# An expert block as one object around the last attention: one batch element's routing computed before the attention's second half, its outputs computed beside the other batch element's norms

## The chip, the core and the metric

The kernel runs on one core of a Trainium2 chip. The metric is the device time in microseconds (us) of one execution. The core has five engines that matter here, each with its own instruction queue that is worked off in order: PE (TensorE: matrix products, weight loads and transposes), DVE (VectorE), ACT (ScalarE), POOL (GpSimd) and SP (which issues most transfers). Engines wait for each other on semaphores.

## What is computed

Eight residual steps over `x` of shape 2 x 512 x 512 (two batch elements of 512 rows). Each step adds a block's output, computed from the layer norm of `x`:

```python
x = x + L0_attn_a(layernorm(x)); x = x + L0_ffn(layernorm(x))
x = x + L0_attn_b(layernorm(x)); x = x + L0_ffn(layernorm(x))
x = x + L1_attn_a(layernorm(x)); x = x + L1_ffn(layernorm(x))
x = x + L1_attn_b(layernorm(x)); x = x + L1_ffn(layernorm(x))
```

The change touches the last three lines' `L1_ffn` (called twice, with the same weights) and the place where `L1_attn_b` is called between the two. `L1_ffn` is a base product plus a mixture of eight experts of rank 16, of which each row takes the best two:

```python
probs = softmax(x_flat @ W_router.T)                  # 8 experts
topk_probs, topk_idx = top_k(probs, 2)
topk_probs = topk_probs / sum(topk_probs)
combine = einsum('nk,nke->ne', topk_probs, one_hot(topk_idx, 8))
h = einsum('nd,erd->ner', x_flat, A)
expert_out = einsum('ner,eor->no', h * combine[:, :, None], B) * 2
out = x_flat @ W_base.T + b_base + expert_out
```

`L1_attn_b` is a causal multi-head attention with 32 heads of 16, with rotary positions, biases and an output product.

## The kernel before

**Tiles.** `x` lies in SBUF as eight tiles `x[0..7]` of 128 rows x 512 (four of batch element 0, four of batch element 1; `NT` is 4, `NTILES` 8). `k.xT[b]` holds the normalised, transposed rows of batch element `b`, from which all products read; it is a part of a tile named `room`. All data are float32, and a float32 matmul stands as two records in the trace.

**Layer norm of one tile** (`layernorm`, lines 171 to 204): DVE takes statistics (L172, L174, L208), POOL makes the inverse square root (L210), DVE writes `xn` (L182), POOL adds the next block's output bias to `x` (L215, where a bias is given), PE makes four transposes into a PSUM bank (L195), and ACT copies the bank into `xT` (L200).

**`ffn_moe`** (line 1310) is called twice, once before the last attention and once after it. It loads its weights (`w` the base weights, 1 MB; `war` the experts' first factors with the router beside them; `wb` the second factors), a bias row and a row `c_order`. For each tile there is a `front` and a `back`:

- `front(t)` (L1339 to L1369): four matmuls of 128 x 136 into a bank of the tag `pj` (there are two such banks), then on DVE the routing: the maximum of the 8 logits (L1345), on ACT the exponential (L1347), and again on DVE two rounds of maximum, comparison, first hit and mask (L1330 to L1336), the renormalisation (L1353 to L1361) and last the product of the 128 expert columns with their weights, `hw` (L1363). That is 16 DVE instructions, nearly all on 8 elements or one per partition, each waiting for the one before. The `pj` bank is read by L1363 and is free only after it.
- `back(t)` (L1371 to L1381): one transpose of `hw` (L1374), an ACT copy `hT` (L1376), four matmuls of 128 x 512 with `w` and one with `wb` into a bank of the tag `sc`, the add to `x[t]` on DVE (L218), and in the last call the transfer of `x[t]` to the output (L1381).

In both calls the loop of lines 1384 to 1393 goes front 0; norm 4; front 1; norm 5, back 0; and so on, so that norms of batch element 1 lie among the fronts of element 0. The norms of element 0 were made before the call.

**`attn_mha`** (line 1479) runs `prepare(b)` and `core(b)` for b = 0, 1. `prepare` makes queries and keys with their rotation (PE, ACT, DVE, POOL, then transfers from `room` into the padded head tiles `qs` and `ks`, L1528) and the values (`values`, L1543, with the DVE add L1547). `core(b)` stands inside a `tc.If` on a register; only its causal branch runs with these inputs. It scores (L1575 on PE, with a maximum on DVE at L1585), transposes the maxima (L1599), scores again transposed (L1611), takes exponentials on ACT (L1621), multiplies by the values (L1636), and ends with the output product (L162) and four adds to `x` (L218). Between `prepare(1)` and `core(1)` the four norms of batch element 0 for the following block are called (lines 1680 to 1683). A `tc.If` is a border for the scheduler: what is called before it stands before it in every engine's queue.

**Order.** A scheduler places the instructions of straight-line parts; within `core` the order on PE is written out by hand. The pools of SBUF: `w8` has five 1 MB buffers, `w3` six smaller ones, `bias` one; the small tiles of `ffn_moe` come from a pool `f1` with three buffers each, opened at each call.

Of the kernel before, what the change touches and what calls it, by code (L numbers as in the profile page):

```python
# [31 lines left out]
F32 = mybir.dt.float32  # L32
# [5 lines left out]
B, S, D = 2, 512, 512  # L38
P = 128
NT = S // P  # L40
# [5 lines left out]
class Block:  # L46


    def __init__(self, ctx, tc, x, out):
        nc = self.nc = tc.nc  # L50
        self.tc = tc
        self.out = out
        pool = lambda name, bufs, **kw: ctx.enter_context(tc.tile_pool(name=name, bufs=bufs, **kw))
        self.const = pool("const", 1)
        self.w = pool("w", 2)
        self.work = pool("work", 2)
        self.small = pool("small", 6)
        self.psum = pool("psum", 2, space=bass.MemoryType.PSUM)
        self.turns = 0
        self.held = None  # L60
        self.coef = None

        self.x = [
            self.const.tile([P, D], F32, tag=f"x{t}", name=f"x{t}") for t in range(NTILES)
        ]
        self.source = x
        self.load_x(0)


        self.room = self.const.tile([P, 4 * KC * S], F32, tag="room", name="room")  # L70
        parts = self.room.rearrange("p (n c s) -> p n c s", n=4, c=KC)
        self.xT = [parts[:, b] for b in range(B)]
        self.spare = [parts[:, 2 + i] for i in range(2)]
        self.spare_turn = 0
        self.ident = self.const.tile([P, P], F32, tag="ident", name="ident")
        make_identity(nc, self.ident)
        self.mhalf = self.const.tile([P, 1], F32, tag="mhalf", name="mhalf")
        nc.gpsimd.memset(self.mhalf, -0.5)
        self.ones = self.const.tile([P, 1], F32, tag="ones", name="ones")
        nc.gpsimd.memset(self.ones, 1.0)  # L80
# [642 lines left out]
class AdaptedBlock:  # L723
# [3 lines left out]
    R = 48  # L727
# [579 lines left out]
        k.release()  # L1307


def ffn_moe(k, a, last=False, beside=lambda t: None):  # L1310

    nc, tc = k.nc, k.tc
    E, R = 8, 16
    with ExitStack() as ctx:
        lp = ctx.enter_context(tc.tile_pool(name="f1", bufs=3))
        w = k.load(a["f1_w"], [P, KC, D], "w8", 5)
        war = k.load(a["f1_ar"], [P, KC, E * R + E], "w3", 6)
        wb = k.load(a["f1_b"], [P, D], "w3", 6)  # L1320
        bias = k.load_row(a["f1_bias"], D, "bias")
        order = k.load_row(a["c_order"], E, "c_order")

        for t in range(NT):
            k.add_bias(t, bias)

        def best(p, name):

            top = k.sm(1, name)
            nc.vector.tensor_reduce(top, p, AX.X, ALU.max)  # L1330
            cand = lp.tile([P, E], F32, tag="cand", name="cand")
            nc.vector.scalar_tensor_tensor(cand, p, top, order, ALU.is_equal, ALU.mult)
            first = k.sm(1, "first")
            nc.vector.tensor_reduce(first, cand, AX.X, ALU.max)
            hot = lp.tile([P, E], F32, tag="hot" + name, name="hot" + name)
            nc.vector.tensor_scalar(hot, cand, first, None, ALU.is_equal)  # L1336
            return top, hot

        def front(t):  # L1339
            b, cols = t // NT, bass.ts(t % NT, P)  # L1340
            ps = k.proj()
            k.chain(ps[:, : E * R + E], [(k.xT[b][:, c, cols], war[:, c]) for c in range(KC)])
            logits = ps[:, E * R : E * R + E]
            nmax = k.sm(1, "nmax")
            nc.vector.tensor_reduce(nmax, logits, AX.X, ALU.max, negate=True)  # L1345
            p = lp.tile([P, E], F32, tag="p", name="p")
            nc.scalar.activation(p, logits, AF.Exp, bias=nmax, scale=1.0)  # L1347
            p1, hot1 = best(p, "p1")
            rest = lp.tile([P, E], F32, tag="rest", name="rest")
            nc.vector.scalar_tensor_tensor(rest, hot1, -2.0, p, ALU.mult, ALU.add)  # L1350
            p2, hot2 = best(rest, "p2")
            both = k.sm(1, "both")
            nc.vector.tensor_tensor(both, p1, p2, ALU.add)  # L1353
            inv = k.sm(1, "inv")
            nc.vector.reciprocal(inv, both)
            c1 = lp.tile([P, E], F32, tag="c1", name="c1")
            nc.vector.tensor_scalar(c1, hot1, p1, None, ALU.mult)
            c2 = lp.tile([P, E], F32, tag="c2", name="c2")
            nc.vector.scalar_tensor_tensor(c2, hot2, p2, c1, ALU.mult, ALU.add)
            comb = lp.tile([P, E], F32, tag="comb", name="comb")  # L1360
            nc.vector.tensor_scalar(comb, c2, inv, 2.0, ALU.mult, ALU.mult)  # L1361
            hw = lp.tile([P, E, R], F32, tag="hw", name="hw")
            nc.vector.tensor_tensor(  # L1363
                hw,
                ps[:, : E * R].rearrange("p (e r) -> p e r", e=E),
                comb.unsqueeze(2).broadcast_to([P, E, R]),
                ALU.mult,
            )
            return hw  # L1369

        def back(t, hw):  # L1371
            b, cols = t // NT, bass.ts(t % NT, P)
            tp = k.tr()
            nc.tensor.transpose(tp[:, :P], hw.rearrange("p e r -> p (e r)"), k.ident)  # L1374
            hT = lp.tile([P, P], F32, tag="hT", name="hT")
            nc.scalar.copy(hT, tp[:, :P])  # L1376
            ps = k.sc()
            k.chain(ps, [(k.xT[b][:, c, cols], w[:, c]) for c in range(KC)] + [(hT, wb)])
            k.add_to_x(t, ps)
            if last:  # L1380
                nc.sync.dma_start(out=k.out[t], in_=k.x[t])  # L1381

        rows = {}
        for t in range(NTILES + 1):
            if t < NTILES:
                rows[t] = front(t)
                beside(t)
            if t < NT:
                k.layernorm(NT + t, bias=bias)
            if t > 0:  # L1390
                back(t - 1, rows.pop(t - 1))
            if t > NT and not last:
                k.layernorm(t - 1 - NT)


class CausalBound:
# [12 lines left out]
    def begin(self, n):  # L1409
        k = self.k  # L1410
        self.w = k.load(self.a["h_w" + n], [P, KC, D], "w8", 5)
        self.row = k.w.tile([P, D], F32, tag="bias", name="bound", bufs=1)
        k.nc.sync.dma_start(out=self.row[:1], in_=self.a["h_r" + n])
# [23 lines left out]
    def end(self):  # L1437
        k, nc = self.k, self.k.nc
        norm = self.norms[0]
        nc.vector.tensor_tensor(norm, norm, self.norms[1], ALU.mult)  # L1440

        nc.vector.tensor_scalar(norm, norm, self.LIMIT, None, ALU.is_lt)
        every = k.sm(1, "ve")[:1]
        nc.vector.tensor_reduce(every, norm, AX.X, ALU.min)
        self.flag = k.const.tile([1, 1], I32, tag="bound_flag", name="bound_flag")
        nc.vector.tensor_copy(self.flag, every)
# [29 lines left out]
        pool.memset(self.nm[i // 4][:, i % 4], 0.0)  # L1476


def attn_mha(k, a, exact, rooms):

# [1 line left out]
    nc, tc = k.nc, k.tc  # L1484
# [4 lines left out]
    with ExitStack() as ctx:  # L1489
        lp = ctx.enter_context(tc.tile_pool(name="h", bufs=2))  # L1490
# [12 lines left out]
        rows = [slice(32 * g, 32 * g + 32) for g in range(4)]  # L1503
# [29 lines left out]
        def prepare(b):  # L1533
            rotated(b, wq, bq, q, (nc.sync, nc.sync))
            if b == 0:
                for t in range(NT, NTILES):
                    k.layernorm(t, bias=bo)
            last = rotated(b, wk, bk, kk, (nc.sync, nc.scalar))

            with tc.issue_after(last):  # L1540
                values(b)
# [136 lines left out]
        for b in range(B):  # L1678
            prepare(b)
            if b:  # L1680

                for t in range(NT):
                    k.layernorm(t)
            with tc.If(exact != 0) as branch:
                core(b, True)
            with branch.Else():
                core(b, False)


@with_exitstack  # L1690
def kernel(ctx: ExitStack, tc: tile.TileContext, a: dict, out: bass.AP):
    k = Block(ctx, tc, a["x"], out)
    k.hold()
    block = attn_latent_small(k, a)
    bound = CausalBound(k, a)
    attn_gqa(k, a, bound, block)
    ffn_lora(k, a)
    attn_mla(k, a)
    with k.tc.tile_pool(name="heads", bufs=1) as pool:
        rooms = HeadRooms(k, a, pool)  # L1700
        ffn_moe(k, a, beside=rooms.fill)
        attn_mha(k, a, bound.register(), rooms)
    ffn_moe(k, a, last=True)

# [154 lines left out]
```

## Time and profile before

| what | value |
|---|---|
| time, three runs | 2104.93, 2110.02, 2113.53 us (median 2110.02) |
| the profiled execution: its own time | 2103.46 us |
| its span, first to last instruction | 2101.4 us |
| mean granted clock of PE | 0.992 |
| PE busy | 2031.9 us (97%) |
| DVE busy | 1351.0 us (64%) |
| ACT, POOL busy | 745.4 us (35%), 970.4 us (46%) |

Busy shares are means over stages that differ; a PE that is busy by its records is not always at its peak. In the views, "idle before <- X" is what ended an engine's wait, the chain of waits is the work that ended last followed back from the last instruction, and the granted clock says which share of full speed PE was given in a stretch. The stages around the change lie as follows in the trace: first expert block 1689 to 1742 us, attention of batch element 0 from 1742 to 1891, `prepare(1)` from 1891 to 1932, `core(1)` from 1935 to 2040, second expert block from 2043 to the end.

### The profile page before, as it was taken

How to read it: one execution, taken by the hardware profiler on the slowest of the kernel's cores; microseconds unless marked ns; L12 is line 12 of the kernel's file. 1: busy time of each engine (PE TensorE's matmuls, PEld its weight loads, DVE VectorE, ACT ScalarE, POOL GpSimd, SP SyncE). 2: the span in 40 equal slices, each digit the busy share in tenths (PEclk: the TensorE clock that was granted, in tenths of full speed). 3: DMA queues.
4: the chain of work that ended last, by engine and by line, in shares of the span. 5: the costliest groups of instructions: out<-in, count | busy, mean ns of one | idle time of the engine just before them, and what ended most of it. 6: DMA issues, size and time to landing. Idle time of an engine off the chain costs nothing. (4 is left out here: it accounts for less than half of the span.)

```text
span 2101.4 us, 40138 instructions
## 1 busy us (share of the span) xinstructions
PE 2031.9 (97%) x15560; PEld 1147.1 (55%) x15560; DVE 1351.0 (64%) x3575; ACT 745.4 (35%) x2072; POOL 970.4 (46%) x1239
## 2 busy tenths in 40 slices
PE   9999999999999999999999989999999999999998
PEld 5444435666666566666665544545454454654654
DVE  7678766756566566666664557666666784855845
ACT  3555632222222222222222145444544411441531
POOL 1101016776555557566653246555555555115220
PEclk9999999999999999999999999999999999999999
DMA  3001012222222222222220321010101003002001
GB/s 100 16 21 41 1 66 76 72 76 71 91 71 71 91 71 76 71 91 76 73 77 26 117 61 54 22 51 25 50 22 52 2 6 70 2 2 41 2 2 40
DMA packets 70221, 107.43 MB, mean 51 GB/s; under 512 B 13699, under 2 KB 50691, under 8 KB 63237
## 3 DMA queue, kind: packets, MB, share of 16 engines
q1 hardware_dynamic: 69380, 103.71, 15.6%
q8 instruction: 126, 2.06, 0.4%
q10 hardware_dynamic: 640, 1.05, 0.3%
q14 instruction: 75, 0.61, 0.1%
HBM read 80.61 MB, written 2.10 MB: 39 GB/s over the span
## 5 line engine op out<-in xcount | busy, mean ns | idle before, releaser
L263 ACT ACTIVATE room<-room,nmax 128x128 f32<-128x128 f32 (+3 forms) x384 | 212.3, 555 | 484.2 <-DVE nmax L253 482.7
L274 POOL TENSOR_SCALAR room<-room,invs 128x128 f32<-128x128 f32 (+3 forms) x384 | 198.0, 537 | 142.1 <-DVE invs L271 142.1
L314 PE MATMUL sc<-turned,vals 32*128 32x128 f32 (+7 forms) x1034 | 186.2, 411 | 1.3 <-DVE turned L287 1.3
L314 PE MATMUL pj<-turned,vals 32*128 32x384 f32 (+7 forms) x708 | 184.9, 422 | 0.0
L210 POOL TENSOR_TENSOR rstd<-ve,mhalf 128x1 f32<-128x1 f32 x80 | 45.9, 577 | 246.0 <-DVE ve L208 240.2
L314 PE MATMUL tp<-turned,vals 32*128 32x256 f32 (+7 forms) x770 | 147.1, 420 | 2.5 <-DMA vals<-v 2.1
L242 PE MATMUL sc<-kT,q 128*32 128x256 f32 (+4 forms) x1528 | 134.0, 384 | 6.8 <-DVE invs L271 4.1
L287 DVE STREAM_TRANSPOSE turned<-room 128x1152 f32<-128x1152 f32 x80 | 109.1, 1363 | 42.4 <-POOL room L274 39.9
L314 PEld LDWEIGHTS sc<-turned,vals 32*128 32x128 f32 (+1 forms) x1034 | 119.3, 166 | 14.3 <-issue 4.2
L943 POOL TENSOR_TENSOR q<-q,cosq 128x512 f32<-128x512 f32 x60 | 89.5, 1491 | 59.9 <-DVE t L940 59.9
L162 PE MATMUL sc<-w,room 128*128 128x512 f32 (+1 forms) x256 | 112.1, 582 | 0.0
L314 PEld LDWEIGHTS pj<-turned,vals 32*128 32x128 f32 (+1 forms) x708 | 104.0, 169 | 4.0 <-issue 1.6
L314 PEld LDWEIGHTS tp<-turned,vals 32*128 32x128 f32 (+1 forms) x770 | 97.6, 169 | 10.8 <-issue 4.9
L162 PE MATMUL sc<-w,ctxT 128*128 128x512 f32 x224 | 101.5, 596 | 0.0
L218 DVE TENSOR_TENSOR x<-sc,x 128x512 f32<-128x512 f32 x79 | 54.2, 686 | 73.0 <-PE sc L162 70.3
L242 PE MATMUL tp<-kT,q 128*32 128x512 f32 (+4 forms) x984 | 91.7, 407 | 4.5 <-DVE invs L271 3.8
L274 POOL TENSOR_SCALAR probs<-probs,invs 128x128 f32<-128x128 f32 (+3 forms) x128 | 65.8, 535 | 65.0 <-DVE invs L271 61.2
L263 ACT ACTIVATE probs<-probs,nmax 128x128 f32<-128x128 f32 (+3 forms) x128 | 71.1, 556 | 65.5 <-DVE nmax L253 64.3
L253 DVE CUSTOM_DVE_ANT_0 room<-sc,mask 128x256 f32<-128x256 f32 (+3 forms) x149 | 70.7, 474 | 35.6 <-PE sc L242 34.1
L242 PE MATMUL pj<-kT,q 128*32 128x288 f32 (+3 forms) x968 | 89.6, 404 | 2.9 <-POOL q L1211 1.9
L944 POOL TENSOR_TENSOR q<-q,t 128x512 f32<-128x512 f32 x64 | 88.0, 1374 | 6.5 <-DVE q L943 2.5
L1208 POOL TENSOR_TENSOR t<-t,sinq 128x512 f32<-128x512 f32 x32 | 40.8, 1276 | 106.4 <-DVE invs L271 100.6
(621 smaller groups left out, 6232.9 us busy)
## 6 DMA issues: line engine op xcount, KB each, us to landing
w<-in_b_wq SPq DMA_DIRECT2D x16, 1024.0 KB, 4.9
w<-in_b_wo SPq DMA_DIRECT2D x16, 1024.0 KB, 5.2
vals<-v SPq DMA_DIRECT2D x256, 64.0 KB, 2.0
w<-in_m_wo SPq DMA_DIRECT2D x8, 1024.0 KB, 7.2
w<-in_b_wk SPq DMA_DIRECT2D x16, 256.0 KB, 2.5
w<-in_b_wupv SPq DMA_DIRECT2D x16, 256.0 KB, 2.5
w<-in_f_w SPq DMA_DIRECT2D x4, 1024.0 KB, 6.0
w<-in_m_wqn SPq DMA_DIRECT2D x8, 384.0 KB, 3.1
```

The source lines that it names most:

```text
L162: last = self.nc.tensor.matmul(out, lhsT, rhs, start=(i == 0), stop=(i == len(pairs) - 1))
L210: self.nc.gpsimd.tensor_tensor(r, ve, self.mhalf, ALU.pow)
L218: self.latest = self.nc.vector.tensor_tensor(self.x[t], ps, self.x[t], ALU.add).ins
L242: nc.tensor.matmul(ps[32 * i : 32 * i + 32, a - lo : b - lo], q[:, at : at + 32], keys[:, a:b], start=True, stop=True,)
L253: nc.vector.tensor_tensor_reduce(out=row, in0=ps[:, :kv], in1=self.mask_back[:, :kv] if qt % 2 else self.mask[:, S - kv :], op0=ALU.add, o ...
L263: nc.scalar.activation(row, row, AF.Exp, bias=nmax, scale=-1.0, accum_out=total[:, qt : qt + 1])
L274: self.nc.gpsimd.tensor_scalar(row, row, inv[:, qt : qt + 1], 1.0, ALU.mult, ALU.mult)
L287: self.nc.vector.transpose(out[:, :last], probs[:, :last])
L314: self.nc.tensor.matmul(out[:, :, :n], values(i, j), rhs, start=(j == blocks[0]), stop=(j == stop[i]),)
L943: mul.tensor_tensor(q, q, tables["cosq"], ALU.mult)
L944: nc.gpsimd.tensor_tensor(q, q, t2, ALU.add)
L1208: nc.gpsimd.tensor_tensor(t2, t2, sinq, ALU.mult)
```

## The change

`ffn_moe` becomes a class `Experts`, built once ahead of both uses, so that the weights, `c_order` and the small tiles live through the attention (pool `f1` now with two buffers each, `hw` with four). Its `front` and `back` are the same instructions as before. `first` is the old first call. The old second call is split: `begin`, called between `prepare(1)` and `core(1)`, makes the norms of batch element 0 as before and directly after each norm its front; `end`, after the attention, makes for each t a norm of element 1, the back of element 0 and the front of element 1, and then the four backs of element 1.

```diff
-def ffn_moe(k, a, last=False, beside=lambda t: None):
...
-        lp = ctx.enter_context(tc.tile_pool(name="f1", bufs=3))
+class Experts:
...
+    def __init__(self, k, a, lp):
...
         w = k.load(a["f1_w"], [P, KC, D], "w8", 5)
         war = k.load(a["f1_ar"], [P, KC, E * R + E], "w3", 6)
         wb = k.load(a["f1_b"], [P, D], "w3", 6)
-        bias = k.load_row(a["f1_bias"], D, "bias")
         order = k.load_row(a["c_order"], E, "c_order")
...
-            hw = lp.tile([P, E, R], F32, tag="hw", name="hw")
+            hw = lp.tile([P, E, R], F32, tag="hw", name="hw", bufs=4)
...
+    def begin(self):
+        self.added = self.bias()
+        for t in range(NT):
+            self.k.layernorm(t, bias=self.added)
+            self.front(t)
+
+    def end(self):
+        for t in range(NT):
+            self.k.layernorm(NT + t, bias=self.added)
+            self.back(t, True)
+            self.front(NT + t)
+        for t in range(NT):
+            self.back(NT + t, True)
...
             prepare(b)
             if b:
-                for t in range(NT):
-                    k.layernorm(t)
+                experts.begin()
...
-    with k.tc.tile_pool(name="heads", bufs=1) as pool:
-        rooms = HeadRooms(k, a, pool)
-        ffn_moe(k, a, beside=rooms.fill)
-        attn_mha(k, a, bound.register(), rooms)
-    ffn_moe(k, a, last=True)
+    with k.tc.tile_pool(name="f1", bufs=2) as own:
+        experts = Experts(k, a, own)
+        with k.tc.tile_pool(name="heads", bufs=1) as pool:
+            rooms = HeadRooms(k, a, pool)
+            experts.first(rooms.fill)
+            attn_mha(k, a, bound.register(), rooms, experts)
+        experts.end()
```

In the built program, PE's queue between the values of `prepare(1)` and the branch into `core(1)` was 16 transposes; it becomes 8 transposes (norms 0 and 1), fronts 0 and 1, 8 transposes (norms 2 and 3), fronts 2 and 3. On DVE the 64 instructions of the four fronts stand directly before that branch, the fronts interleaved in pairs (0 with 1, then 2 with 3). After the attention PE's queue becomes: transposes of norm 4, back 0, front 4, transposes of norm 5, back 1, front 5, and so on, and at the end backs 4 to 7. On SP the second loads of `w`, `war`, `wb` and `c_order` are gone; the row `h_bv` moves two places up. POOL's queue has the same instructions in the same order.

In the old code the norms between the halves were called without a bias, and the bias was added to `x[0..3]` at the head of the second `ffn_moe` (lines 1324 and 1325); now the norm adds it. The scheduler had put these four adds at the same place in POOL's queue in both kernels.

More of the change, by code (lines that the diff above doesn't have):

```diff
@@ L1307, in attn_mla @@
         k.release()
-def ffn_moe(k, a, last=False, beside=lambda t: None):
-    nc, tc = k.nc, k.tc
-    E, R = 8, 16
-    with ExitStack() as ctx:
-        lp = ctx.enter_context(tc.tile_pool(name="f1", bufs=3))
+class Experts:
+    def __init__(self, k, a, lp):
+        nc = k.nc
+        E, R = 8, 16
+        self.k, self.a = k, a
+        self.rows = {}
         w = k.load(a["f1_w"], [P, KC, D], "w8", 5)
@@ L1320, in ffn_moe @@
         wb = k.load(a["f1_b"], [P, D], "w3", 6)
-        bias = k.load_row(a["f1_bias"], D, "bias")
         order = k.load_row(a["c_order"], E, "c_order")
-        for t in range(NT):
-            k.add_bias(t, bias)
         def best(p, name):
@@ L1368, in front, with back @@
             )
-            return hw
-        def back(t, hw):
+            self.rows[t] = hw
+        def back(t, last):
+            hw = self.rows.pop(t)
             b, cols = t // NT, bass.ts(t % NT, P)
@@ L1381, in back, with bias, first @@
                 nc.sync.dma_start(out=k.out[t], in_=k.x[t])
-        rows = {}
+        self.front, self.back = front, back
+    def bias(self):
+        return self.k.load_row(self.a["f1_bias"], D, "bias")
+    def first(self, beside):
+        k, bias = self.k, self.bias()
+        for t in range(NT):
+            k.add_bias(t, bias)
         for t in range(NTILES + 1):
             if t < NTILES:
-                rows[t] = front(t)
+                self.front(t)
                 beside(t)
@@ L1390, in ffn_moe @@
             if t > 0:
-                back(t - 1, rows.pop(t - 1))
-            if t > NT and not last:
+                self.back(t - 1, False)
+            if t > NT:
                 k.layernorm(t - 1 - NT)
+    def begin(self):
+        self.added = self.bias()
+        for t in range(NT):
+            self.k.layernorm(t, bias=self.added)
+            self.front(t)
+    def end(self):
[3 more added lines that the diff above has]
+            self.front(NT + t)
+        for t in range(NT):
+            self.back(NT + t, True)
 class CausalBound:
@@ L1476, in fill, with attn_mha @@
         pool.memset(self.nm[i // 4][:, i % 4], 0.0)
-def attn_mha(k, a, exact, rooms):
+def attn_mha(k, a, exact, rooms, experts):
     nc, tc = k.nc, k.tc
@@ L1680, in attn_mha @@
             if b:
-                for t in range(NT):
-                    k.layernorm(t)
+                experts.begin()
             with tc.If(exact != 0) as branch:
```

## The prediction

> **What bounds the kernel now.** I read the page first: PE is busy 97% and DVE 64%, a mean over stages, so it says only that a change is worth what it takes off or puts onto PE's queue in the two places it touches. Those are the last block (from 2040 us) and the start of `core(1)` (at 1935 us).
>
> The chain of waits over the last block (start, length, what):
>
> ```profile
> 2039.78 0.70 DVE x L218
> 2040.48 2.10 issue
> 2042.58 0.70 DVE ln_stats L172
> ...
> 2044.97 1.27 POOL x L215
> ...
> 2049.26 0.17 DVE nmax L1345
> ...
> 2053.81 1.16 DVE comb L1361
> ...
> 2055.44 0.30 PE tp L1374
> 2055.74 4.27 PE sc L162 x6
> 2060.02 0.93 PE pj L162 x8
> 2060.94 0.44 PE tp L195 x4
> 2061.49 4.29 PE sc L162 x10
> ...
> 2097.38 0.69 DVE x L218
> ```
>
> After the attention's last add (2040.48) a norm must be made before PE gets work (2044.95); then PE waits for the routing of the first two fronts until 2055.44. From there PE is dense: a tile with back, front and norm transposes takes 5.77 us (2060.78 to 2066.55 between the norm transposes of two tiles), a back alone 4.40 (between the last two, 2088.30 to 2092.71). PE ends at 2097.1.
>
> The stretches, with busy time of PE, PEld, DVE, ACT, POOL, then the granted clock:
>
> ```profile
> 1936.00:1943.00 7.00, 4.63 (x31) 3.16 (x25) 7.00 (x32) 0.00 (x0) 0.38 (x1) 1.00 0.00 1
> 1943.00:1947.00 4.00, 4.00 (x30) 3.29 (x31) 3.92 (x20) 0.29 (x1) 0.00 (x0) 0.57 0.02 4
> 2045.00:2049.00 4.00, 3.92 (x17) 3.32 (x18) 2.94 (x9) 0.00 (x0) 3.34 (x4) 0.57 0.00 0
> 2055.40:2059.00 3.60, 3.56 (x6) 1.53 (x7) 2.04 (x12) 0.27 (x1) 0.00 (x0) 0.55 0.00 0
> ```
>
> Two things stand here. After a gap, PE runs some 4 us at little over half clock (last two rows). And the first 7 us of `core(1)` are DVE's: it is busy 7.00 of 7.00 with the score maxima, while PE is not. A delay of DVE's first maximum there delays everything behind it.
>
> **The change, part by part.**
>
> *Weights kept.* The second load of the base weights (1 MB) goes. It was issued 300 us before its use, so nothing waited for it:
>
> ```profile
> 1740.21 0.33 SPq L110 DMA_DIRECT2D w<-in_f_w  x1
> 1759.18 0.33 SPq L116 DMA_DIRECT2D bias<-in_f_bias  x1
> ```
>
> Worth 0. The bias row is still loaded by `begin`, behind the same users of the one `bias` buffer, and the `h_bv` row, which moves up, now waits for tiles of the attention before, which end by 1689; its first reader is at 1775 (L1547). If either were late, POOL's adds would be: the room is over 50 us. The pool of two buffers instead of three, and `hw` of four, in the first expert block: PE's and DVE's orders are unchanged there and each tile's reader precedes its next writer by a whole tile (5.3 us); 0.
>
> *The tail.* PE's queue now holds, after the transposes of norm 4, a back whose `hw` has long been there. PE still begins at 2044.95, since the norm of element 1 needs the attention's last adds and stands first in the queue. Its work from there: four tiles of 5.77 us (norm transposes, back, front) and four backs of 4.40, 23.1 + 17.6 = 40.7 us. One cold start: 4.0 us at 0.57 loses 4.0 x 0.43 = 1.7. Does anything stop it? Front 4's routing is needed only four tiles later; the next norm's `xn` (2047.3 before) is needed at about 2052; `hT` is an ACT copy of 0.27 us beside 3.4 us of matmuls. So PE ends at 2044.95 + 40.7 + 1.7 = 2087.3 in place of 2097.1: **-9.8 us**. What follows the last matmul (add, transfer, end: 4.3 us) stays. Bounds: -11.5 if PE were granted full clock at once; -7 if waits of 1.4 us as in the first block (PE at 1714.74, before a `hw`) came twice.
>
> *The middle.* The four fronts are not new work, but they now stand on DVE directly before the branch into `core(1)`, so its first maximum waits for all 64 of their instructions. Nothing hides them: DVE cannot start earlier, because the fronts need PE's transposes, which stand behind the values, and later in the queue is the DVE-paced stretch above. The rows:
>
> ```profile
> 1933.65 2.73 POOL L215 TENSOR_TENSOR x<-x,bias 128x512 f32<-128x512 f32 x2 [8.61 <-DVE xn L182]
> 1935.66 0.30 DVE L1585 CUSTOM_DVE_ANT_0 tp<-tp,mask 128x128 f32<-128x128 f32 x1 [1.63 <-PE pj L1575]
> 2051.01 1.19 DVE L1350 SCALAR_TENSOR_TENSOR rest<-hotp,p 128x8 f32<-128x8 f32 x1
> 2072.51 0.17 DVE L1345 TENSOR_REDUCE nmax<-pj 128x1 f32<-128x8 f32 x1 [0.23 <-PE pj L162]
> 2075.73 0.29 DVE L1363 TENSOR_TENSOR hw<-pj,comb 128x128 f32<-128x128 f32 x1
> ```
>
> One front alone takes 2072.51 to 2076.02, 3.5 us. The order interleaves two. I laid the second chain into the first's gaps with the spacings of that front (0.2 to 0.27 us between dependent instructions, 0.1 between independent ones): the first `hw` ends 3.8 us after the start, the second at 5.3. POOL's two bias adds run until 1936.38; instructions like L1350 then stretch from 0.17 to 1.19 (third row), so +0.9 for the first pair. Walking it: norm 0's copy is done at 1933.4, front 0's matmuls (0.93) at 1934.4, L1345 at 1934.5; the two `hw` at 1939.2 and 1940.7. Fronts 2 and 3 need the two `pj` banks that these free. PE has idled 3 us by then, so I take the half-clock duration of such a front (1.96 us, at 2045.44): front 2 ready at 1941.2, front 3 at 1943.1. The second pair: 1941.3 + 5.3, and 0.6 for front 3 being late: 1947.2. The first maximum follows 0.2 later (0.16 in `core(0)`, at 1786.06), at 1947.4 in place of 1935.66: **+11.7 us**. The transfers into `ks`, last issued at 1930.95 with 3.7 to 4.8 us to landing, are in by then and cost nothing. Behind the waiting DVE stand the maxima, behind them PE's transposes of maxima and all of `core(1)`, whose first eight scores fill the banks and then wait too. PE's cold clock at that point is again covered by DVE's pace, as at 1943 now. Bounds: +9.6 (both pairs 5.3, no hold, full clock) and +19.0 (pairs as slow as the first expert block's, 1690.36 to 1700.06 = 9.7 us, where POOL fills rooms beside them).
>
> [...]
>
> *Sum:* +11.7 - 9.8 = **+1.9 us**. The profiled execution took 2103.46 us (span 2101.4), so 2105.4 by its own measure; it lies 6.6 us under the median of the three runs, 2110.0. On the median's scale: **2112 us**, 0.1% above. A measurement of this kernel can tell about 0.5% (10.5 us; the three runs lie 8.6 apart), so this is no change: a gain at the end paid back in the middle.
>
> **The rivals.**
>
> *A, slower: the middle costs twice what I say.* Place: DVE between 1934 and the first maximum. If the fronts interleave as poorly as in the first expert block (9.7 us a pair), or the bank hand-off makes the second pair wait out the first, the delay is 19.0 and more: two pairs of 9.7, 2.2 of hand-off with a cold PE, 0.2: 1956.3, +20.6. With -9.8: +10.8, 2121. It is slower at all from a pair of 4.4 us on, and beyond 0.5% from pairs of about 9.7. For: those 9.7 were measured on the same instructions. Against: there norms stood between the fronts and POOL worked without a break; here POOL is idle from 1936.4.
>
> *B, faster: the middle is mostly hidden.* If `core(1)` took up the delay, because its later units leave PE or DVE room, only part of the 11.7 would reach the end; at 2 us left, -7.8: 2102; at none, 2100. For: PE idles in the first row above. Against: from 1953 on PE is busy 6.93 of 7 us, and its queue is written by hand, so lost time is not made up.
>
> *C: the tail doesn't gain.* PE's queue has norm transposes before each back; if each waited for its norm as the first does, backs would start late and only the routing wait's half, some 4 us, would be saved: +7.7, 2118. Against: all four norms' statistics were done by 2049.4 before, two of them while PE worked.
>
> **How the numbers follow.** Forecast 0.55, A 0.25, B 0.14, C 0.06. The likeliest's own range, from the bounds (+9.6 - 11.5 to +11.7 - 7), is 2108 to 2115. Reaching toward A and B, and with the runs' own scatter of some 4 us: 2101 to 2123. Faster by over 0.5% (under 2099.5) needs B whole and a little more: 0.10. Slower by over 0.5% (over 2120.6): most of A and some of C, 0.27. Within: 0.63.
>
> **What would show it.** In the profile after: the first score maximum of `core(1)` (L1585 before) at about 1947 us, with DVE's small routing instructions solid from 1934.5 before it; the attention's last add near 2051.5; PE then starting 4.5 us after that add with one cold stretch and no gap over 1 us to the end; about 51 us from the end of that add to the end of the span, where it was 60.9. Wrong would be a first maximum before 1944 or after 1951, a PE gap beside a `hw` in the tail, or a span that changes before 1930.

## The result, and the profile after

The changed kernel took 2107.44 us (median of 12 runs, 2102.83 to 2110.9), the kernel before 2108.18 (12 runs on the same chip, 2104.6 to 2113.53): ratio 0.9996, 95% interval 0.9984 to 1.0008. That is no change, as forecast, and 2107.44 lies inside the stated 2101 to 2123. The profiled execution after took 2106.94 us with a span of 2105.2, 3.8 us more than the one of before; 2.25 us of that lies ahead of the fronts (the adds of the values, L1547 before and L1572 after, end that much later), and it is the scatter of single executions: the last key activation in `prepare(1)`, ahead of the fronts too, starts at 1918.70 us before and at 1920.95 after, but at 1918.48 and 1918.35 in two kernels below whose code is the changed kernel's up to there (middle alone, other banks). So the prediction's warning sign of a span that changes before 1930 is met in this one execution without anything behind it.

The middle. The timeline of DVE at the last add of the values before (start, length, line, operation, out<-in, and in brackets what ended the idle time ahead of it):

```profile
1932.43 0.69 DVE L1547 TENSOR_TENSOR vs<-sc,h_bv 128x512 f32<-128x512 f32 x1 [2.74 <-PE sc L162]
```

After, from the last add of the values to the first score maximum:

```profile
1934.68 0.69 DVE L1572 TENSOR_TENSOR vs<-sc,h_bv 128x512 f32<-128x512 f32 x1 [2.74 <-PE sc L162]
...
1936.99 0.17 DVE L1344 TENSOR_REDUCE nmax<-pj 128x1 f32<-128x8 f32 x1 [0.70 <-PE pj L162]
...
1937.69 0.97 DVE L1331 SCALAR_TENSOR_TENSOR cand<-p,p,c_order 128x8 f32<-128x8 f32 x1
...
1942.44 0.29 DVE L1362 TENSOR_TENSOR hw<-pj,comb 128x128 f32<-128x128 f32 x1
1942.64 0.15 DVE L1344 TENSOR_REDUCE nmax<-pj 128x1 f32<-128x8 f32 x1
...
1947.57 0.29 DVE L1362 TENSOR_TENSOR hw<-pj,comb 128x128 f32<-128x128 f32 x1
1947.81 0.30 DVE L1610 CUSTOM_DVE_ANT_0 tp<-tp,mask 128x128 f32<-128x128 f32 x1
```

The first maximum stands directly behind the last `hw`, with no wait: DVE's routing chain sets it, in two pairs of 5.74 us (1936.99 to 1942.73) and 5.22 us (1942.64 to 1947.86). From the last add of the values to the maximum it is 13.13 us, where it was 3.23 (1932.43 to 1935.66): the middle costs 9.9 us.

PE in the same stretch, with the products of the fronts (0 and 1 in the first row, then 2, then 3):

```profile
1935.76 2.12 PE L162 MATMUL pj<-w,room 128*128 128x136 f32 x16 [0.24 <-ACT room L200]
...
1941.42 1.16 PE L162 MATMUL pj<-w,room 128*128 128x136 f32 x8 [2.67 <-DVE cand L1331]
1942.88 1.16 PE L162 MATMUL pj<-w,room 128*128 128x136 f32 x8 [0.29 <-DVE nmax L1344]
```

PE waits 2.67 us for the first bank, as foreseen, but then does a front in 1.16 us, not in the 1.96 that the prediction took from a row at half clock. Front 2 is there before DVE wants it.

The tail. Before, PE waited 4.92 us for routing ahead of its first back:

```profile
2055.44 0.30 PE L1374 MATMUL tp<-ident,hw 128*128 128x128 f32 x1 [4.92 <-DVE first L1334]
```

After, in the chain of waits:

```profile
2052.67 0.70 DVE x L218
2053.37 2.10 issue
2055.47 0.71 DVE ln_stats L172
...
2057.84 1.11 PE tp L195 x4
2058.95 0.21 PE tp L1374
2059.17 6.34 PE sc L162 x10
2065.51 0.93 PE pj L162 x8
2066.44 0.44 PE tp L195 x4
2066.87 0.11 PE tp L1374
2066.98 4.29 PE sc L162 x10
...
2097.06 4.31 PE sc L162 x10
...
2101.46 0.69 DVE x L218
```

Behind norm 4's transposes the back's transpose (L1374) starts at once, and from there to 2101.37 PE is the chain without a break. The wait for routing is gone; what is left is one stretch at a low clock (1.11 for the four transposes that take 0.44 later, 6.34 for the ten products that take 4.29). The windows (busy time of PE, PEld, DVE, ACT, POOL, then the granted clock):

```profile
2057.84:2062.00 4.16, 4.16 (x9) 2.47 (x10) 3.10 (x9) 0.75 (x2) 3.48 (x4) 0.50 0.02 4
2062.00:2066.00 4.00, 4.00 (x13) 1.94 (x12) 1.13 (x4) 0.00 (x0) 2.11 (x3) 0.85 0.00 0
2066.00:2070.00 4.00, 4.00 (x17) 2.33 (x17) 3.25 (x12) 0.99 (x3) 1.27 (x1) 1.00 0.17 66
```

For all runs together the stage is best cut at four marks: the last key activation on ACT in `prepare(1)`, the first score maximum, the attention's last add (the start of each), and the end of the span.

| kernel | key to maximum | maximum to add | add to end | ratio to before, 95% interval |
|---|---|---|---|---|
| before | 16.96 | 104.12 | 61.62 | 1 |
| after | 26.86 | 104.86 | 52.53 | 0.9996 (0.9984 to 1.0008) |
| weights kept alone | 16.96 | 105.77 | 62.35 | 0.9997 (0.9983 to 1.001) |
| middle alone | 27.75 | 104.84 | 62.13 | 1.0058 (1.0036 to 1.008) |
| tail alone | 16.96 | 105.78 | 52.63 | 0.9948 (0.9929 to 0.9967) |
| GpSimd busy | 35.33 | 104.35 | 52.41 | 1.0038 (1.0024 to 1.0051) |
| other banks | 25.70 | 104.19 | 51.96 | 0.998 (0.9967 to 0.9992) |
| fronts early | 23.01 | 105.10 | 52.88 | 0.9977 (0.9964 to 0.999) |
| early, keys by SyncE | 20.40 | 104.92 | 52.74 | 0.9961 (0.9947 to 0.9976) |
| dense order | 21.37 | 104.85 | 52.23 | 0.997 (0.9958 to 0.9982) |
| dense, two bias adds gone | 19.80 | 104.29 | 52.16 | 0.9959 (0.9944 to 0.9973) |

The first segment repeats to 0.01 us where nothing in it changed; the attention between scatters by 1.7 us in kernels whose attention is the same.

### The profile page after: what moved, and what is told of

Same layout as the page of the kernel before. It is cut to its first block, busy times and chain, and to the rows that moved or that the text cites. A ratio compares the mean times of both kernels' runs of the same rounds, so it can differ in the third digit from the quotient of the medians.

```text
span 2105.2 us, 40131 instructions
## 1 busy us (share of the span) xinstructions
PE 2036.7 (97%) x15560; PEld 1149.4 (55%) x15560; DVE 1349.8 (64%) x3575; ACT 745.4 (35%) x2072; POOL 969.4 (46%) x1239
```

## The experiments

**The three parts one by one.** Weights kept: the class stays, `begin` makes only norms, `end` has the old loop.

```diff
             self.k.layernorm(t, bias=self.added)
-            self.front(t)
...
     def end(self):
-        for t in range(NT):
...
+        for t in range(NTILES + 1):
+            if t < NTILES:
+                self.front(t)
+            if t < NT:
+                self.k.layernorm(NT + t, bias=self.added)
+            if t > 0:
+                self.back(t - 1, True)
```

> The class with weights loaded once and two buffers in its pool is kept; the norms alone stand between the last attention's halves and all eight fronts stand in the last block, in the old loop's order. My theory: the reload was off the path, so this is the kernel before: ratio 1.000, within 0.002; first score maximum of core(1) at 1935.7 and 60.9 us from the end of the attention's last add to the end of the span. Rival 'the weights kept pay' (or cost): a change of over 4 us (ratio under 0.998 or over 1.002), and the other parts would then not add up without it.

Measured 0.9997, and a first segment of 16.96 us, the same as before: neither loading the weights once nor the pool's buffers is worth anything that shows, with about 3 us to either side.

Middle alone: `begin` as in the changed kernel, `end` with the old loop as above, so that four fronts are made twice.

> The four fronts stand ahead of the branch as in the changed kernel, and the last block makes all eight fronts again as before, so the first four are made twice: the middle's cost alone. My theory: first maximum of core(1) some 10 us later (1945.5 to 1948), all of it still there at the attention's last add, tail 60.9 us as before: +10.6 us, ratio 1.005. Rival B, the attention takes up the delay: first maximum as late, but the last add late by 2 us at most, ratio 1.001 or less. Rival A, the middle costs 19 or more: ratio 1.009 and above.

Measured 1.0058: +12.2 us by 2105.64, with 4.6 us to either side. The first maximum came 10.8 us later, the tail stayed. Nothing of the delay was made up: from the key activation to the last add it is 132.6 us, before 121.1, which is 11.5 more. Rival B falls. This middle is 0.9 us dearer than that of the changed kernel, with the same instructions; its PE and DVE rows say why:

```profile
1938.96 3.50 PE L162 MATMUL pj<-w,room 128*128 128x136 f32 x16 [2.67 <-DVE cand L1331]
```

```profile
1941.15 0.17 DVE L1344 TENSOR_REDUCE nmax<-pj 128x1 f32<-128x8 f32 x1 [0.89 <-PE pj L162]
```

After the same wait of 2.67 us the fronts 2 and 3 took 3.50 us together, and DVE waited 0.89 for them. The windows over the stretch and the start of `core(1)` (busy time of PE, PEld, DVE, ACT, POOL, then the granted clock) of the changed kernel:

```profile
1936.00:1943.00 7.00, 4.04 (x33) 3.67 (x33) 5.55 (x34) 1.79 (x6) 2.64 (x2) 1.00 0.03 7
1943.00:1947.00 4.00, 1.79 (x18) 1.50 (x22) 3.58 (x28) 0.43 (x2) 0.00 (x0) 1.00 0.00 0
1948.00:1953.00 5.00, 4.99 (x25) 4.39 (x25) 5.00 (x25) 0.00 (x0) 0.00 (x0) 0.50 0.02 3
```

and of the middle alone:

```profile
1936.00:1943.00 7.00, 4.21 (x23) 3.67 (x21) 5.43 (x39) 1.74 (x5) 0.17 (x1) 0.76 0.00 1
1943.00:1947.00 4.00, 1.91 (x14) 1.37 (x15) 3.84 (x31) 0.03 (x1) 0.00 (x0) 0.78 0.00 0
```

The clock was granted in full in the one (and was 0.50 from 1948 on) and fell within the stretch in the other. What makes it fall early or late wasn't tried.

Tail alone: no fronts in the middle, and `end` as in the changed kernel; the routed expert outputs of batch element 0 are left out.

```diff
             self.k.layernorm(t, bias=self.added)
-            self.front(t)
+            hw = self.blank()
+            self.rows[t] = hw
```

> The middle makes only the norms, and the routed weights of the first batch element's four tiles are set to zero in GpSimd (the routing and the expert outputs of those tiles are left out); the last block is that of the changed kernel: the tail's gain alone. My theory: first maximum and last add as in the kernel before (1935.7 and 2039.8), then some 52 us to the end in place of 60.9: -9.1 us, ratio 0.9957. Rival C, the tail doesn't gain because its backs wait for norms: 57 us or more from the last add, -4 or less, ratio 0.998 or above. Together with the kernel that has the middle alone, the two should add up to about +1.5.

Measured 0.9948 (-10.9 us by the runs, -9.0 by the last segment). Rival C falls. Middle and tail alone add up to 1.0058 - 0.0052 = 1.0006, within the interval of the changed kernel (the sum's own interval is about 0.003 to either side): the result is a gain of some 10 us at the end paid back in the middle.

**Rival A's condition made on purpose.**

```diff
             self.k.layernorm(t, bias=self.added)
+            if t == NT - 1:
+                self.busy(t, 12)
             self.front(t)
...
+        def busy(t, n):
+            s = k.work.tile([P, D], F32, tag="xn", name="xn")
+            for i in range(n):
+                nc.gpsimd.tensor_tensor(s, k.x[t], k.x[t], ALU.add)
```

> The changed kernel with twelve additions of 128x512 on GpSimd, whose result nobody uses, behind its last bias add, so that GpSimd works beside the second pair of fronts, as it does in the first expert block. Rival A's condition made on purpose. My theory: instructions of three operands on VectorE stretch beside GpSimd as the one at 1937.69 did (0.97 in place of 0.23); with some eight to twelve such in the second pair, it takes 9 to 11 us in place of 5.2, first maximum 4 to 6 us later, ratio to the kernel before about 1.002. If GpSimd isn't what made the pairs of the first block take 9.7 us, the second pair stays at 5.2 us and the ratio at 0.9995.

Measured 1.0038. The adds ran earlier than I had laid them, from 1939.18 on and so beside the first pair, which took 13.2 us (1937.45 to 1950.67) in place of 5.74; the second took 6.2, and the maximum came 8.5 us later than in the changed kernel. POOL, then DVE:

```profile
1939.18 13.37 POOL L1386 TENSOR_TENSOR xn<-x 128x512 f32<-128x512 f32 x12
```

```profile
1946.12 0.87 DVE L1331 SCALAR_TENSOR_TENSOR cand<-rest,p,c_order 128x8 f32<-128x8 f32 x1
...
1947.22 0.89 DVE L1335 TENSOR_SCALAR hotp<-cand,first 128x8 f32<-128x8 f32 x1
1948.15 1.08 DVE L1358 SCALAR_TENSOR_TENSOR c<-hotp,p,c 128x8 f32<-128x8 f32 x1
1949.26 1.08 DVE L1360 TENSOR_SCALAR comb<-c,inv 128x8 f32<-128x8 f32 x1
```

These four take 0.22 or 0.23 us elsewhere. They end at 1946.99, 1948.11, 1949.23 and 1950.34, which is 1.11 to 1.12 us apart: POOL's own step, 13.37 / 12 = 1.11, by which its seventh to tenth add end at an estimated 1946.98, 1948.09, 1949.21 and 1950.32. Each of these four thus waited for the end of a whole GpSimd instruction, one for each; the reductions between them keep their 0.14 to 0.17 us. So rival A was a real mechanism and only its condition, a busy GpSimd, was absent. The first expert block's own rows show such instructions (`cand` 1.17 us at 1693.72, `c` 1.19 at 1698.14, before), but how much of its 9.7 us a pair is due to them wasn't tried.

**The bank hand-off.** Fronts 2 and 3 in banks of other tags.

```diff
-            self.front(t)
+            self.front(t, (k.proj, k.proj, k.av, k.sc)[t])
```

> The changed kernel with fronts 2 and 3 in banks of the weighted sums and the scores, so that TensorE need not wait for fronts 0 and 1 to give back theirs. The term of the prediction that measured smallest: the hand-off at a cold clock, 1.5 us in the sum. My theory: what the hand-off cost was 0 to 0.9 us, by where the clock stood (the 16 matmuls took 2.3 us in the changed kernel's profile and 3.5 in that of the middle alone), so the second pair starts without a gap and the first maximum is 0 to 1.5 us earlier; no more, since VectorE's chain is what sets it: ratio 0.999 to 0.9995. Rival: the hand-off is the middle's main cost, and the first maximum moves by 3 us or more.

The first maximum came 1.2 us earlier, within what I gave it, and the rival of 3 us or more falls: DVE's chain, not the banks, is most of the middle. The timed ratio, 0.998, is lower than that accounts for.

**A better place for the fronts.** Here the norms and fronts are interleaved with the values on PE (norms 0, 1; values 0; fronts 0, 1; values 1; norms 2, 3; values 2; fronts 2, 3; values 3), so that DVE's chain has PE work beside it. The values call a step ahead of each of their four products:

```diff
+        def step(t):
+            k = self.k
+            if t % 2 == 0:
+                k.layernorm(t, bias=self.added)
+                k.layernorm(t + 1, bias=self.added)
+            else:
+                self.front(t - 1, k.av if t > 1 else k.proj)
+                self.front(t, k.sc if t > 1 else k.proj)
...
-                values(b)
+                if b == 0:
+                    values(b)
+                else:
+                    with tc.manual_schedule(engines={mybir.EngineType.PE}):
+                        values(b, experts.begin())
...
-            if b:
-                experts.begin()
```

> The changed kernel with its fronts moved ahead: on TensorE's queue the norms, the fronts and the values of the second half are interleaved (norms 0, 1; values 0; fronts 0, 1; values 1; norms 2, 3; values 2; fronts 2, 3; values 3), fronts 2 and 3 in banks of the weighted sums and the scores, so that the routing's chain on VectorE runs beside TensorE's values and doesn't wait for the banks of fronts 0 and 1. My theory: what was lost in the middle was a chain of small VectorE instructions with nothing beside it; half or more of it hides, first maximum at 1938 to 1942, tail as in the changed kernel: -4 to -7 us against the kernel before, ratio 0.997. Rival: VectorE's own work up to the branch is the limit, or the values' adds are pushed back behind the fronts, and the first maximum stays at 1945 or later: ratio 0.9995 as the changed kernel.

Measured 0.9977: the kernel is now some 5 us faster than the one before. Its interval still touches that of the changed kernel, but its first segment is 3.85 us shorter. The maximum is 6.05 us later than before, at the worse end of the 2.3 to 6.3 expected. ACT's timeline shows the loss:

```profile
1927.46 3.50 ACTq L1561 DMA_DIRECT2D ks<-room  x4
1931.01 0.42 ACT L1346 ACTIVATE p<-pj,nmax 128x8 f32<-128x8 f32 x2 [10.95 <-issue]
```

The maxima of fronts 0 and 1 were ready at 1924, but their exponentials stood on ACT behind four transfer issues, which wait for GpSimd's last room (its end at 1927.43, the first issue at 1927.46). With those issues on SyncE:

```diff
-            last = rotated(b, wk, bk, kk, (nc.sync, nc.scalar))
+            last = rotated(b, wk, bk, kk, (nc.sync, nc.sync if b else nc.scalar))
```

> The kernel with the fronts moved ahead, in which the exponentials of fronts 0 and 1 waited on ScalarE from 1924 to 1931 behind its own four transfer issues into ks, which wait for GpSimd's last room; here SyncE issues all eight. My theory: the exponentials run at 1924 to 1926, fronts 0 and 1 are done on VectorE by 1931 beside the values, and the first maximum comes 2 to 3 us earlier than in the kernel with the fronts moved ahead: -7 us against the kernel before, ratio 0.9965. Rival: the transfers into ks then land later than the first scores want them, and nothing is gained or some us lost: ratio 0.9977 or above.

```profile
1924.18 0.27 ACT L1346 ACTIVATE p<-pj,nmax 128x8 f32<-128x8 f32 x1 [3.79 <-DVE nmax L1344]
```

The exponential runs at 1924.18, the first segment shrinks by 2.6 us, and the ratio is 0.9961. Not all of that is ACT's: with the issues on ACT, the routing stood on DVE behind the add of values 2 too (1932.31; its first instruction ran at 1932.92, 1.5 us after the exponentials were done), and with the issues moved the scheduler put it ahead of that add (1924.48). Then a denser order, with all statistics first and fronts 2, 3 ahead of values 2:

```diff
+            if t in (1, 2):
+                self.front(2 * t - 2, k.av if t > 1 else k.proj)
+                self.front(2 * t - 1, k.sc if t > 1 else k.proj)
...
+            if t == NT - 1:
+                with k.tc.issue_after(ended):
+                    for i in range(NT):
+                        k.add_bias(i, self.added)
```

> As the last, with all that the fronts need still earlier: statistics of all four norms first, TensorE's order norms 0, 1; values 0; fronts 0, 1; norms 2, 3; values 1; fronts 2, 3; values 2, 3, and the four bias adds on GpSimd behind its last room. My theory: only TensorE's own 3.7 us for the fronts is left in the middle, first maximum about 3 us later than in the kernel before: 3 - 9.1 = -6 to -8 us, ratio 0.9967. Rival: VectorE's routing instructions, put before the adds of values 2 and 3 and beside GpSimd, or the transfers into ks, set the first maximum, and it is no better than the kernel with the fronts moved ahead: ratio 0.9977.

The rival's mechanism was there, though not its whole price: +4.4 us at the maximum in place of 3, which is 1.6 better than the fronts moved ahead and 1.0 worse than the same with SyncE; the ratio, 0.997, can't tell it from either, and by the runs its -6.3 us lie inside my -6 to -8. The four bias adds, held back behind GpSimd's last room, now ran from 1924.82 to 1929.76, beside the first pair, which took 8.8 us. Asked for at the head of the last block instead (the scheduler still puts two of them behind the last room):

```diff
     def end(self):
+        for t in range(NT):
+            self.k.add_bias(t, self.added)
```

> The densest order with the four bias adds asked for at the head of the last block; two of them then run on GpSimd long before the fronts and two still behind its last room, at some 1925 to 1927.5. My theory: VectorE's three-operand instructions wait for whole GpSimd instructions, as beside the twelve added ones, so the first pair, stretched from 5.2 to 8.7 us in the densest order by four adds, is stretched by some 1.7 only; then TensorE's end of the values and VectorE's two adds behind it set the first maximum, some 20 us after the last key activation in place of 21.4: -7 to -8.5 us against the kernel before, ratio 0.9963. Rival: something else held the densest order, and it stays at 21.4 and 0.997.

The first pair is down to 6.7 us (1924.42 to 1931.11), the first segment to 19.80, 2.8 more than before, where PE's own time for four fronts is 3.7 (4 x 0.93); ratio 0.9959. This is the best of the kernels that do the whole work, some 8.6 us under the kernel before, though its interval and that of the simpler order with SyncE overlap almost whole.

## Why the prediction was right

**The sum: +1.9.** The segments of the two profiles give +9.9 - 9.1 = +0.8, the timed runs -0.8 with some 2.5 to either side. Both parts are there, each close to its size; the middle was taken 1.8 too high and the tail's gain 0.7 too high, and that these two cancel in part is luck. The forecast of 2112 also stood on a median of three runs, 2110.02, where twelve give 2108.18.

**Weights kept: 0.** The run that has them alone shows nothing, within its 3 us.

**The tail: -9.8, measured -9.1** (61.62 to 52.53). PE starts 4.47 us after the end of the last add, to the hundredth as before, no wait follows, and the tiles take 5.77 and the backs 4.40. The mis-sized term is the one cold start: I took 1.7 us lost; the four transposes lose 0.67, the back's transpose 0.10, the ten products 2.05, together 2.8, since the granted clock was 0.50 up to 2062 and still 0.85 on the mean from there to 2066, where I took 4.0 us at 0.57. The end behind the last matmul was 0.5 us shorter than the 4.3 taken; 0.2 of that is the reading of PE's end before, which the last row of the chain puts at 2097.29 and not at 2097.1.

**The middle: +11.7, measured +9.9, and +10.8 where it stood alone.** Place and mechanism were right: DVE's chain, two pairs, then the first maximum at once. Most of the error is in the step "Fronts 2 and 3 need the two `pj` banks", where I put a half clock on PE. Term by term in the changed kernel: the first pair starts 0.2 us later than laid out, and takes 5.74 in place of 6.2; the gap between the pairs, taken as 0.6, is none; the 0.6 for a late front 3 is not there, the second pair taking 5.22 in place of 5.9; and the 0.2 ahead of the maximum is not there. That half clock wasn't there in the changed kernel's profile; in that of the middle alone it came (3.50 us for both), cost 0.89, and still didn't stretch the second pair (5.14).

Counting by the rows of one front (3.5 us for its sixteen instructions) was the right choice. The 64 instructions took 10.87 us, from 1936.99 to 1947.86, of which some 0.75 is the wait for GpSimd (0.97 us at 1937.69 in place of 0.22). Little of it is idle time: by its records DVE is busy for 9.60 of the 10.87 us. The length lies in the spacing from start to start, 0.19 to 0.27 us where an instruction needs the one before and mostly 0.06 to 0.14 where the two chains interleave.

**The rivals.** A had a quarter of the chance; its price is real (8.5 us when GpSimd works beside the fronts) and its condition wasn't met: GpSimd's two bias adds reach one instruction of the first pair (0.97 us at 1937.69). B fell, for the reason given: later units made nothing up. C fell: no back waited for a norm.

**Open.** The timed runs of the kernels with the new tail lie some 1 to 3 us below what their first and last segments add up to against the one profile of before (the changed kernel -0.8 for +0.8, other banks -4.2 for -0.9, the best -8.6 for -6.6). The scatter of the attention between, and the intervals of about 2 to 4 us to either side, are of that size, but the sign is the same each time. Part of it is the one profile of before: the two kernels that keep the old tail took 62.35 and 62.13 us from the last add, 0.5 to 0.7 more than its 61.62, and the difference lies mainly in PE's first stretch after its wait (6.26 and 6.11 us from the transpose of `hw` to the next norm's transposes, 5.50 before). The kernel with the weights kept alone shows the same gap without the new tail (-0.6 by the runs for +0.7). What the rest is wasn't settled.

## What to carry to other kernels

Moving a chain of small dependent instructions costs nearly its whole length where nothing stands beside it (here a chain of 10.87 us cost 9.9): look for a place where the engine that waits for it has other work queued, and count the chain by measured spacings, not by busy time. When such a chain is moved, look at what stands ahead of each of its steps on every queue: here four transfer issues on ScalarE, with the order on VectorE that came with them, cost 2.6 us, and GpSimd work at the same moment up to 8.5. Test the two halves of a change alone before calling it worthless: one was worth 10 us, and the other could be made to cost 3 in place of 10.

## What the runs showed of the hardware

Beside the twelve added GpSimd instructions, some VectorE instructions on 128 x 8 elements (`cand`, `hotp`, `c`, `comb`) waited for the end of a running GpSimd instruction: 0.22 or 0.23 us became 0.8 to 1.1, ending in step with GpSimd's 1.11 us, while the reductions beside them (0.14 to 0.17 us) never stretched in that run. `hotp`, which reads one tensor and one scalar for each partition, waited (0.89 us at 1947.22) as `cand` did, which reads two tensors and one such scalar (0.87 us at 1946.12). What in the hardware makes them wait wasn't shown.

The granted clock after the same 2.67 us of idling was full (1.00 from 1936 to 1943, the changed kernel) in one execution and 0.76 on the mean (the same window, the middle alone) in another. One execution of each is too few for a rate, but they show that a low clock behind so short a wait isn't a fixed cost.
